# Layer norm of a transformer block moved to ScalarE, in program order, with earlier requests for the tokens

## The chip, the cores and the metric

The kernel runs on one core of a Trainium2 chip. The core has TensorE (matrix products, called PE in the profile; PEld are its weight loads), VectorE (DVE), ScalarE (ACT), GpSimd (POOL) and SyncE (SP, which issues most of the transfers). Each engine works through its own list of instructions in order and waits on semaphores for the others. The metric is the device time of one execution in microseconds (us), lower is better.

## The reference

One block of a diffusion transformer, in fp32, on 2 rows of 2048 tokens with 512 features, 16 heads, and 2048 hidden features of the MLP. A condition vector gives each row six modulation vectors.

```
mod = silu(condition) @ Wada + bada
sh_a, sc_a, gt_a, sh_m, sc_m, gt_m = split(mod, 6)
xn = layernorm(x, g1, be1)
xm = xn * (1 + sc_a) + sh_a
x  = x + gt_a * (causal_attention(xm @ Wqkv) @ Wproj + bproj)
xn = layernorm(x, g2, be2)
xm = xn * (1 + sc_m) + sh_m
x  = x + gt_m * (gelu(xm @ W1 + b1) @ W2 + b2)
```

`layernorm` subtracts each token's mean over the 512 features, divides by the root of the variance plus 1e-5, and applies g and be.

## The kernel before, in words

The work runs in stages, and for the two rows one after the other: QKV of row 0, attention of row 0, projection of row 0, then the same for row 1, then the MLP of both rows. In the profiled execution QKV of row 0 takes the time from about 20 to 200 us, its attention to 740, its projection to 799, row 1's QKV to 997, its attention to 1530, its projection to 1590, and the MLP the rest. A stage does some work of the next beside its own, through hooks called `between(n)` after each product `n`.

**Tokens on their way to QKV.** A tile `x` holds 128 tokens by 512 features; four tiles make a group of 512 tokens, and a row has four groups. The pool of a row's `x` tiles has four buffers, so one group's. `load_x` requests the four tiles of a group on SP's queue. `stats` runs two VectorE instructions for a tile (L215, L218: mean and variance into `mv`). After the fourth, `inv_std` makes `rstd` of a group: a root on ScalarE (L221), a reciprocal on VectorE (L222). `norm(g, j)` takes the two tiles of half `j` of group `g`: it normalizes each in place on VectorE (L244, subtract the mean, multiply by `rstd`), transposes the 128 x 128 blocks on TensorE into PSUM banks `ps_xt` (L211), and writes them with scale and shift of the modulation into `xmT` (L263 on VectorE, L268 on ScalarE, by turns). The reference's normalized and modulated tokens are then in `xmT`, features along the partitions.

**The products of a QKV group.** `Qkv.group` runs 12 products: eight for queries and keys (n = 0 to 7; a q and a k product for each quarter of the features), four for values (n = 8 to 11). After a q or k product ScalarE writes a rounded copy `hl` of the result (L833), VectorE the remainder (L834), and SP stores both parts to DRAM (`q<-hl`, `k<-hl`, L839). The text calls these two instructions the split. `hl` has four buffers; one comes free when its store has landed. After a value product ScalarE copies the result to `vv` (L855). Products and transposes take their PSUM banks from one pool of six.

**What runs beside it.** From the second group on, scores of the first units of attention are computed among the products (matmuls into `s`, from `qst` and `kst`, which SP loads back from the stores), and VectorE takes their maxima (`mx`, L456 and L461). `s` has two banks, so a score matmul waits for the maximum taken from the bank it will fill. In row 1's QKV stage GpSimd also prepares the MLP's weights (`w`, `w1e`, `w2d`), with loads and stores of its own.

**What sets the order.** Instructions wrapped in `act(...)` or `mm(...)`, matrix products and transposes among them, keep the order of the program on their engine. All others a scheduler places on their engine, ahead of or behind these, when it expects their operands. The normalizes of `norm` are not wrapped, and of the statistics only those called with `keep`. When group `g` runs, `between` requests group `g + 1`'s tokens at n = 0 (unless already there) and calls `norm(g + 1, 0)` at n = 5 and `norm(g + 1, 1)` at n = 8. In row 0 for every group after the first, and in row 1 for its third and fourth, `norm(g, 0)` runs the four statistics ahead of the normalizes. Row 1's first two groups have theirs from the projection of row 0.

**Hooks of the two projections.** `project_phase` runs 16 products of a row's attention output with Wproj. While row 0's runs, its hook makes row 1's first group ready: statistics at n = 0 to 3, `norm` at n = 5 and 8. While row 1's runs, the hook makes the first two groups of the MLP ready: `ln_t` (normalize and transpose, with `mv2` and `rstd2`) at n = 5, 7, 11 and 13. These tiles carry the name `qst` in the profile. The MLP's later groups are normalized on ScalarE already (L1281, `xn<-x,shift,rstd`), with `shift2` = -mean x rstd made at the end of `project_phase` (L1064).

The call that puts everything the scheduler does for a group into one place:

```
def norm(self, g, j):
    if j == 0:
        if g > b:
            for t in range(MTT):
                self.stats(g, t)
        self.xmT[g] = ...
    return transposed(...)
```

Of the kernel before, what the change touches and what calls it, by code (L numbers as in the profile page):

```python
# [17 lines left out]
P = 128  # L18
# [9 lines left out]
def dit_block_kernel(  # L28
# [36 lines left out]
    nc = tc.nc  # L65
# [82 lines left out]
    rstd1 = const.tile([P, B * NT], F32, tag="rstd1", name="rstd1")  # L148
    mv2 = const.tile([P, B * NT, 2], F32, tag="mv2", name="mv2")
    rstd2 = const.tile([P, B * NT], F32, tag="rstd2", name="rstd2")  # L150
    shift2 = const.tile([P, B * NT], F32, tag="shift2", name="shift2")

    bgate = bp.tile([P, D], F32, tag="bgate", name="bgate")
# [51 lines left out]
    def act(ins):  # L205

        return tc.keep_in_program_order(ins)
# [9 lines left out]
            act(ins)  # L217
        nc.vector.bn_aggr(mv[:, n, :], st)  # L218

    def inv_std(mv, rstd, lo, hi):  # L220
        nc.scalar.activation(rstd[:, lo:hi], mv[:, lo:hi, 1], AF.Sqrt, bias=eps)  # L221
        nc.vector.reciprocal(rstd[:, lo:hi], rstd[:, lo:hi])  # L222

    def rows_of(psum, r, b, tag):

# [1 line left out]
        mm(ps, pick[:, r, b, :], modr, start=True, stop=True)  # L227
        return ps

    def transposed(pool_, psum, xts, n0, mv, rstd, a, c, b, dst, xns=None):  # L230

        count = len(xts)
        per = 512 // (count * P)
        by_act = xns is not None
        xns = xns or []
        for t, xt in enumerate(xts):
            if by_act:  # L240
                continue
            xn = xt
            n = n0 + t
            nc.vector.tensor_scalar(  # L244
                xn, xt, mv[:, n, 0:1], rstd[:, n : n + 1], ALU.subtract, ALU.mult
            )
            xns.append(xn)
        banks = []
        for cc in range(0, C, per):
            ps = psum.tile([P, per, count * P], F32, tag="mm", name="ps_xt")  # L250
            for ci in range(per):
                for t in range(count):
                    transpose(
                        ps[:, ci, t * P : (t + 1) * P],
                        xns[t][:, (cc + ci) * P : (cc + ci + 1) * P],
                    )
            banks.append(ps)

        def modulate(chunks=range(C)):
# [12 lines left out]

        return modulate
# [498 lines left out]
    class Qkv:  # L772
# [20 lines left out]
        def stats(self, g, t, keep=False):  # L793

            n0 = self.row.b * NT + g * MTT
            stats(self.qp, self.xts[g][t], n0 + t, mv1, keep)
            if t == MTT - 1:
                inv_std(mv1, rstd1, n0, n0 + MTT)

        def norm(self, g, j):  # L800

            b = self.row.b
            if j == 0:
                if g > b:
                    for t in range(MTT):
                        self.stats(g, t)
                self.xmT[g] = self.qp.tile([P, C, MT], F32, tag="xmT", name="xmT", bufs=2)
            return transposed(
                self.qp, self.psum, self.xts[g][2 * j : 2 * j + 2],
                b * NT + g * MTT + 2 * j, mv1, rstd1, a1, c1, b,  # L810
                self.xmT[g][:, :, j * 2 * P : (j + 1) * 2 * P],
            )

# [45 lines left out]
        def run(self, hp, also):  # L859

            row = self.row
            for g in range(NG):

                def between(n):
                    if g + 1 < NG:
                        if n == 0 and g + 1 not in self.xts:
                            self.load_x(g + 1)
                        if n in (5, 8):
                            self.norm(g + 1, n // 8)()
                    elif n == 8:  # L870

                        row.rows(0)
                        act(nc.scalar.activation(first, eps, AF.Exp))
                    also(g, n)

                def among(n, k):
                    if g > 0 and n >= 2:


                        past = 4 * (n - 2) + k + 1  # L880
                        if g == 1:
                            row.score(row.count(cum[0] * past / 40, 0))
# [119 lines left out]
    def project_phase(row, psum, between):  # L1002
# [5 lines left out]
        with pool(f"proj{b}") as pp:  # L1008
# [51 lines left out]
                    between(n)  # L1060
                    n += 1
        lo, hi = b * NT, (b + 1) * NT
        inv_std(mv2, rstd2, lo, hi)
        nc.vector.scalar_tensor_tensor(  # L1064
            shift2[:, lo:hi], mv2[:, lo:hi, 0], -1.0, rstd2[:, lo:hi], ALU.mult, ALU.mult
        )


    row = Row(0)
    with pool("wada") as wp, pool("qkv0") as qp, pool(  # L1070
# [87 lines left out]

        for t in range(MTT):
            qkv.stats(0, t)  # L1160
        halves = [qkv.norm(0, 0)]

        act(
# [3 lines left out]
        )  # L1167
        picks()
        columns = modulation(0)
        halves.append(qkv.norm(0, 1))  # L1170
        columns()
        scale_shift(a1, c1, r_g1, r_be1, 0, 1)
# [36 lines left out]
    with pool("qkv1") as qp, pool("ps_qkv1", bufs=6, space=PSUM) as ps_mm:  # L1209
        qkv = Qkv(row, qp, ps_mm)  # L1210
        qkv.xts[0] = past.next_s

        def between(n):
            if n == 6:
                qkv.load_w(nc.gpsimd)

            if n < MTT:
                qkv.stats(0, n, True)
            if n in (5, 8):
                qkv.norm(0, n // 8)()  # L1220
            if n == 8:
                qkv.load_x(1)
            if n >= NT - MTT:
                qkv.stats(1, n - (NT - MTT), True)

        project_phase(past, ps_mm, between)

        with pool("hl1") as hp:
            late = FirstLayer(hp)

            def also(g, n):
                if quarters.at <= FC:
                    if n % 2 == 1:
                        quarters.step()
                elif n % 2 == 0:
                    late.step()

            def rooms():
                w = hp.tile([P, 7, C * P], F32, tag="w49", name="w7", bufs=2)
                w = w.rearrange("p n d -> p (n d)")  # L1240
                return [w[:, k * piece : (k + 1) * piece] for k in range(2)]

            quarters.more_rooms = rooms
            qkv.run(hp, also)
            assert quarters.at >= FC and late.at == 7 and not late.rooms
# [8 lines left out]
    with ExitStack() as mlp:  # L1254
# [8 lines left out]
        ]  # L1263
        sx = {}

        def ln_t(m, g, j, xts, xns=None):

            n0 = (2 * m + g) * MTT + 2 * j
            transposed(
                wp, ps_mm, xts, n0, mv2, rstd2, a2, c2, n0 // NT,  # L1270
                xm[:, :, g, j * half_t : (j + 1) * half_t], xns,
            )()

        def normed(m, n, xts):
# [106 lines left out]
        def between(n):  # L1381
            if n == 4:
                gate_columns()
            if n in (6, 7):
                wts.load(0, n - 6)
            if n in (5, 7):
                j = n // 7
                ln_t(0, 0, j, row.next_s[2 * j : 2 * j + 2])
                for t in (2 * j, 2 * j + 1):
                    nc.sync.dma_start(row.next_s[t], x1d[MTT + t])  # L1390
            if n in (11, 13):
                j = n // 13
                ln_t(0, 1, j, row.next_s[2 * j : 2 * j + 2])
            if n == 13:
                for k in range(1, 5):
                    token_sum(k)
# [440 lines left out]
        for m in range(NM):  # L1837
# [11 lines left out]
            if m + 1 < NM:  # L1849
# [11 lines left out]
                def among(n, k):  # L1861
                    n = OUTER.index(n)
                    if n < MTT and k == 3:
                        xns.append(normed(m + 1, n, coming[0]))
                    elif n < MTT and k == 6:
                        if n + 1 < MTT:
                            coming.append(load_pair(n + 1))
                        ln_t(m + 1, n // 2, n % 2, coming.pop(0), xns.pop())
                    elif n == 6 and k >= 3:
                        assert not hid.todo  # L1870
                        token_sum(k - 2)
# [56 lines left out]
```

## Time and profile before

| | us |
|---|---|
| median of 3 runs | 2316.29 |
| lowest and highest of them | 2315.68, 2319.18 |
| the profiled execution's own time | 2323.64 |
| its span, first to last instruction | 2321.8 |

The profile is of one execution. Durations and idle times in it add up to its span, not to the median of the other runs. A row of a timeline or of a group reads: start and duration (or busy time and mean), engine, line of the code, operation, output and inputs by their names in the program, shapes, how many, and in brackets the idle time of the engine ahead of it with what ended it. A row of the waits reads: engine, tile and line that waited, then engine, tile and line it waited for, then the time in all, how often, and the longest. A row of the windows reads: the stretch, its length, then busy time and number of instructions of TensorE, weight loads, VectorE, ScalarE and GpSimd, the granted TensorE clock as a share of full speed, the share of time that the DMA engines are busy (1.00 is all 16; a little more can come out) and GB/s.

### The profile page before, as it was taken

To read this page: it belongs to the slowest core of one execution; us is meant where nothing else is said; L and a number is where in the kernel's file an instruction comes from. 1 tells how busy PE (TensorE), PEld (TensorE's weight loads), DVE (VectorE), ACT (ScalarE), POOL (GpSimd) and SP (SyncE) were. 2 spreads that over 40 slices of the span, in tenths; PEclk is the share of its full clock that TensorE was granted. 3 is DMA by queue.
4 is the path that set the end of the run, shared out by engine and by line. 5 is a ranking of instruction groups with operands and counts; after the bars stand their busy time and mean duration, and the time that the engine had idled before them with its cause. 6 is when DMAs were issued, how large, how long until landed. Compare 5 with 4: busy or idle time off the path is not lost. (4 is left out here: it accounts for less than half of the span.)

```text
span 2321.8 us, 33418 instructions
## 1 busy us (share of the span) xinstructions
PE 2262.0 (97%) x12141; PEld 1387.3 (60%) x12141; DVE 1579.0 (68%) x3117; ACT 915.0 (39%) x1744; POOL 1289.6 (56%) x1036
## 2 busy tenths in 40 slices
PE   8999999999999999999999998999999999999998
PEld 3455455455544444454455554446888888788787
DVE  3366776777756635577677777555896876876787
ACT  2112555555555011155555554622332242152230
POOL 1052987878793664468788885554663602602510
PEclk9999999999999999999999999999999999999999
DMA  7577216151224799970522304265376654654543
GB/s 254 185 243 206 56 27 134 29 119 47 84 107 144 234 301 312 330 192 24 119 47 54 89 24 138 78 218 203 119 266 214 207 178 145 202 184 155 199 143 116
DMA packets 118524, 355.60 MB, mean 153 GB/s; under 512 B 14496, under 2 KB 15052, under 8 KB 103640
## 3 DMA queue, kind: packets, MB, share of 16 engines
q1 hardware_dynamic: 107040, 293.64, 42.0%
q0 software_dynamic: 10944, 59.28, 7.0%
q8 instruction: 96, 1.57, 0.3%
q14 instruction: 68, 0.56, 0.1%
q10 hardware_dynamic: 376, 0.55, 0.1%
HBM read 253.80 MB, written 107.48 MB: 156 GB/s over the span
## 5 line engine op out<-in xcount | busy, mean ns | idle before, releaser
L596 ACT ACTIVATE e<-st 128x512 f32<-128x512 f32 (+1 forms) x1152 | 573.7, 579 | 405.5 <-PE st L203 363.6
L461 DVE TENSOR_REDUCE mx<-s 128x1 f32<-128x512 f32 x612 | 413.4, 687 | 190.3 <-PE s L203 189.1
L626 POOL TENSOR_TENSOR ee<-ee,e 128x1024 f32<-128x1024 f32 x212 | 498.8, 2384 | 12.3 <-ACT e L596 12.3
L203 PE MATMUL s<-kst,qst 128*128 128x512 f32 (+3 forms) x1032 | 473.6, 460 | 20.7 <-DVE mx L461 9.9
L203 PE MATMUL st<-qst,kst 128*128 128x512 f32 (+3 forms) x1280 | 401.9, 379 | 0.0
L203 PE MATMUL ps_a<-sum,room 128*128 128x256 f32 x1504 | 357.3, 382 | 8.8 <-DVE c L1412 6.2
L203 PEld LDWEIGHTS ps_a<-sum,room 128*128 128x128 f32 x1504 | 281.3, 190 | 58.5 <-issue 11.4
L203 PE MATMUL o<-e,vv 128*32 128x512 f32 (+3 forms) x2560 | 301.1, 539 | 0.9 <-POOL e L605 0.9
L456 DVE CUSTOM_DVE_ANT_0 junk<-s,causal 128x128 bf16<-128x128 f32 (+3 forms) x420 | 206.2, 491 | 121.8 <-PE s L203 114.1
L203 PEld LDWEIGHTS s<-kst,qst 128*128 128x128 f32 x1032 | 194.6, 189 | 154.8 <-issue 66.1
L203 PEld LDWEIGHTS st<-qst,kst 128*128 128x128 f32 x1280 | 229.5, 189 | 68.9 <-issue 39.6
L626 POOL TENSOR_TENSOR ee<-e 128x1024 f32<-128x1024 f32 x84 | 198.2, 2381 | 123.2 <-ACT e L596 123.2
L203 PE MATMUL ps_qk<-xmT,wqkv 128*128 128x512 f32 x512 | 239.0, 594 | 1.8 <-DVE xmT L263 1.8
L605 POOL TENSOR_SCALAR_AFFINE_SELECT e<-e 128x256 f32<-128x256 f32 x256 | 103.9, 435 | 112.5 <-ACT e L596 110.3
L203 PEld LDWEIGHTS ps_qk<-xmT,wqkv 128*128 128x128 f32 x512 | 93.9, 190 | 97.2 <-issue 90.9
L203 PEld LDWEIGHTS <-sel 32*128 32x128 bf16 x1152 | 29.8, 91 | 197.0 <-issue 194.9
L1640 POOL TENSOR_TENSOR c<-c,h 128x512 f32<-128x512 f32 x40 | 58.0, 1470 | 160.8 <-ACT c L1638 160.8
L203 PE MATMUL ps_b<-sum,room 128*128 128x256 f32 x608 | 143.6, 379 | 0.0
L203 PEld LDWEIGHTS ps_b<-sum,room 128*128 128x128 f32 x608 | 115.0, 190 | 15.4
L203 PE MATMUL ps_v<-wqkv,xmT 128*128 128x512 f32 x256 | 123.7, 600 | 0.0
L203 PE MATMUL st<-fold,sel 32*128 32x512 bf16 (+1 forms) x1152 | 118.5, 373 | 4.3 <-DVE mhl L482 2.8
L203 PEld LDWEIGHTS o<-e,vv 128*32 128x32 f32 x2560 | 61.3, 108 | 98.9 <-issue 80.8
(179 smaller groups left out, 2949.5 us busy)
## 6 DMA issues: line engine op xcount, KB each, us to landing
qst<-q SPq DMA_DIRECT2D x128, 256.0 KB
room<-w1e SPq DMA_DIRECT2D x28, 1024.0 KB
kst<-k SPq DMA_DIRECT2D x24, 1024.0 KB
room<-w1e SPq DMA_DIRECT2D x28, 768.0 KB
room<-w2e SPq DMA_DIRECT2D x21, 1024.0 KB
q<-hl SPq DMA_DIRECT2D x32, 512.0 KB
k<-hl SPq DMA_DIRECT2D x32, 512.0 KB
room<-w2e SPq DMA_DIRECT2D x21, 768.0 KB
```

The lines of the kernel that those rows point to most:

```text
L203: return tc.keep_in_program_order(nc.tensor.matmul(*args, **kw))
L456: nc.vector.tensor_tensor_reduce(junk[:, :w], s[:, :w], causal[:, QB - w :], 1.0, MASKED, ALU.add, ALU.max, m,)
L461: nc.vector.tensor_reduce(m, s[:, :w], axis=AX.X, op=ALU.max)
L596: act(nc.scalar.activation(e[:, h % 2, :w], sts[h][:, :w], AF.Exp))
L605: nc.gpsimd.affine_select(d, d, pattern=[[0, 2], [1, P]], compare_op=ALU.is_ge, fill=0.0, base=0, channel_multiplier=-1,)
L626: act(engine.tensor_tensor(dst, x, y, ALU.add))
L1640: nc.gpsimd.tensor_tensor(c, c, piece_of(base, i, t, pair), ALU.add)
```

## The change

- A new constant `shift1` holds -mean x rstd for the first norm. `inv_std` makes it with one more VectorE instruction for each group (for the MLP's norm the instruction that made `shift2` moves into `inv_std`).
- A new function `normalize` does what `transposed` did ahead of its transposes, wrapped in `act`. It uses ScalarE (in place, Identity with `shift` as bias and `rstd` as scale), except for row 0's first group, which stays on VectorE. So 36 of 40 normalizes change engine.
- Within a QKV group the four statistics of the next group come one after each of the products 1 to 4, wrapped too. The normalizes follow at n = 5 and 8, the transposes one product later than before, at n = 6 and 9.
- The tokens of group g + 2 are requested at n = 9 of group g, in place of n = 0 of group g + 1.
- In row 0's projection the normalizes stand at n = 4 and 7, the transposes as before at 5 and 8. In row 1's the normalizes stand at n = 4, 6, 10 and 12, the transposes as before at 5, 7, 11 and 13.
- In the MLP only the arguments of `ln_t` change.

```diff
-    def inv_std(mv, rstd, lo, hi):
+    def inv_std(mv, rstd, lo, hi, shift=None):
         nc.scalar.activation(rstd[:, lo:hi], mv[:, lo:hi, 1], AF.Sqrt, bias=eps)
         nc.vector.reciprocal(rstd[:, lo:hi], rstd[:, lo:hi])
+        if shift is not None:
+            nc.vector.scalar_tensor_tensor(
+                shift[:, lo:hi], mv[:, lo:hi, 0], -1.0, rstd[:, lo:hi], ALU.mult, ALU.mult
+            )
...
+    def normalize(xts, n0, mv, rstd, shift):
+        for t, xt in enumerate(xts):
+            n = n0 + t
+            if shift is None:
+                act(
+                    nc.vector.tensor_scalar(
+                        xt, xt, mv[:, n, 0:1], rstd[:, n : n + 1], ALU.subtract, ALU.mult
+                    )
+                )
+            else:
+                act(
+                    nc.scalar.activation(
+                        xt, xt, AF.Identity,
+                        bias=shift[:, n : n + 1], scale=rstd[:, n : n + 1],
+                    )
+                )
...
-            nc.vector.tensor_scalar(
-                xn, xt, mv[:, n, 0:1], rstd[:, n : n + 1], ALU.subtract, ALU.mult
-            )
...
         def norm(self, g, j):
             b = self.row.b
             if j == 0:
-                if g > b:
-                    for t in range(MTT):
-                        self.stats(g, t)
...
                         if n == 0 and g + 1 not in self.xts:
                             self.load_x(g + 1)
+                        if 1 <= n <= MTT and g >= row.b:
+                            self.stats(g + 1, n - 1, True)
                         if n in (5, 8):
-                            self.norm(g + 1, n // 8)()
+                            self.normalize(g + 1, n // 8)
+                        if n in (6, 9):
+                            self.norm(g + 1, n // 9)()
+                        if n == 9 and g + 2 < NG:
+                            self.load_x(g + 2)
...
+            if n in (4, 7):
+                qkv.normalize(0, n // 7)
             if n in (5, 8):
                 qkv.norm(0, n // 8)()
...
+            if n in (4, 6, 10, 12):
+                g, j = n // 10, int(n in (6, 12))
+                normalize(
+                    row.next_s[2 * j : 2 * j + 2], g * MTT + 2 * j, mv2, rstd2, shift2
+                )
```

More of the change, by code (lines that the diff above doesn't have):

```diff
@@ L150, in dit_block_kernel @@
     rstd2 = const.tile([P, B * NT], F32, tag="rstd2", name="rstd2")
+    shift1 = const.tile([P, B * NT], F32, tag="shift1", name="shift1")
     shift2 = const.tile([P, B * NT], F32, tag="shift2", name="shift2")
@@ L228, in rows_of, with transposed @@
         return ps
-    def transposed(pool_, psum, xts, n0, mv, rstd, a, c, b, dst, xns=None):
-        count = len(xts)
-        per = 512 // (count * P)
[L237 to L244, printed above, removed]
-                xn, xt, mv[:, n, 0:1], rstd[:, n : n + 1], ALU.subtract, ALU.mult
-            )
-            xns.append(xn)
+    def normalize(xts, n0, mv, rstd, shift):
[14 more added lines that the diff above has]
+                )
+    def transposed(psum, xns, a, c, b, dst, by_act=False):
+        count = len(xns)
+        per = 512 // (count * P)
         banks = []
@@ L797, in stats, with normalize @@
             if t == MTT - 1:
-                inv_std(mv1, rstd1, n0, n0 + MTT)
+                inv_std(mv1, rstd1, n0, n0 + MTT, shift1)
+        def normalize(self, g, j):
+            b = self.row.b
+            normalize(
+                self.xts[g][2 * j : 2 * j + 2], b * NT + g * MTT + 2 * j,
+                mv1, rstd1, shift1 if b or g else None,
+            )
         def norm(self, g, j):
@@ L803, in norm @@
             if j == 0:
-                if g > b:
-                    for t in range(MTT):
-                        self.stats(g, t)
                 self.xmT[g] = self.qp.tile([P, C, MT], F32, tag="xmT", name="xmT", bufs=2)
             return transposed(
-                self.qp, self.psum, self.xts[g][2 * j : 2 * j + 2],
-                b * NT + g * MTT + 2 * j, mv1, rstd1, a1, c1, b,
+                self.psum, self.xts[g][2 * j : 2 * j + 2], a1, c1, b,
                 self.xmT[g][:, :, j * 2 * P : (j + 1) * 2 * P],
@@ L1062, in project_phase @@
         lo, hi = b * NT, (b + 1) * NT
[L1063 to L1066, printed above, removed]
+        inv_std(mv2, rstd2, lo, hi, shift2)
     row = Row(0)
@@ L1160, in dit_block_kernel @@
             qkv.stats(0, t)
+        qkv.normalize(0, 0)
         halves = [qkv.norm(0, 0)]
@@ L1169, in dit_block_kernel @@
         columns = modulation(0)
+        qkv.normalize(0, 1)
         halves.append(qkv.norm(0, 1))
@@ L1264, in dit_block_kernel, with ln_t @@
         sx = {}
-        def ln_t(m, g, j, xts, xns=None):
+        def ln_t(m, g, j, xns, by_act=False):
             n0 = (2 * m + g) * MTT + 2 * j
             transposed(
-                wp, ps_mm, xts, n0, mv2, rstd2, a2, c2, n0 // NT,
-                xm[:, :, g, j * half_t : (j + 1) * half_t], xns,
+                ps_mm, xns, a2, c2, n0 // NT,
+                xm[:, :, g, j * half_t : (j + 1) * half_t], by_act,
             )()
@@ L1385, in between @@
                 wts.load(0, n - 6)
+            if n in (4, 6, 10, 12):
+                g, j = n // 10, int(n in (6, 12))
+                normalize(
+                    row.next_s[2 * j : 2 * j + 2], g * MTT + 2 * j, mv2, rstd2, shift2
+                )
             if n in (5, 7):
@@ L1867, in among @@
                             coming.append(load_pair(n + 1))
-                        ln_t(m + 1, n // 2, n % 2, coming.pop(0), xns.pop())
+                        coming.pop(0)
+                        ln_t(m + 1, n // 2, n % 2, xns.pop(), True)
                     elif n == 6 and k >= 3:
```

## The prediction

> **What bounds the kernel now.** I read the page's engine totals first, then TensorE's waits, then the windows around them, and last the instructions at each wait.
>
> ```profile
> PE 2262.0 (97%) x12141; PEld 1387.3 (60%) x12141; DVE 1579.0 (68%) x3117; ACT 915.0 (39%) x1744; POOL 1289.6 (56%) x1036
> ...
> PE 27%; DVE 4%; issue 1%; ACT 0%; DVEq 0%; ACTq 0%
> ```
>
> TensorE is busy for 97% of 2321.8 us and leads the chain that ended last. The change takes no matmul away, so it can only win what TensorE idles, 59.8 us in all, and of this only the part in stages that the change touches. VectorE's average of 68% says little; what counts is where it is late.
>
> ```profile
> 840.00:860.00 20.00, 17.85 (x46) 8.04 (x45) 9.82 (x27) 3.16 (x6) 10.69 (x17) 1.00 0.99 310
> 860.00:880.00 20.00, 20.00 (x66) 10.33 (x64) 7.27 (x23) 4.41 (x8) 13.47 (x20) 1.00 1.05 314
> 880.00:900.00 20.00, 17.39 (x45) 8.11 (x44) 10.98 (x32) 3.63 (x7) 7.44 (x11) 1.00 0.85 273
> 900.00:920.00 20.00, 20.00 (x64) 10.66 (x63) 13.74 (x34) 3.41 (x6) 7.69 (x8) 1.00 0.92 303
> 920.00:940.00 20.00, 17.21 (x51) 8.95 (x50) 11.12 (x29) 3.18 (x6) 10.02 (x10) 0.91 1.03 364
> ...
> PE s L203 <- DVE mx L461: 5.4, 2, 2.8
> PE s L203 <- DVE mx L456: 2.1, 1, 2.1
> ```
>
> The windows give TensorE, weight loads, VectorE, ScalarE and GpSimd busy time, then the granted clock, the DMA share and GB/s; the last two rows are TensorE's waits from 795 to 1005 us, the QKV stage of row 1. It has three holes of 2.15, 2.61 and 2.79 us, and in each a score matmul waits for a maximum on VectorE. The other windows are full. In row 0's QKV stage no such hole stands: there the change has nothing to win, only room to lose.
>
> **The change part by part.** *Statistics one a product, and no normalize on VectorE.* The first two holes:
>
> ```profile
> 847.44 0.69 DVE L215 BATCH_NORM_STATS2 stat<-x 128x6 f32<-128x512 f32 x1 [9.05 <-DMA x<-in_x_dram]
> 848.05 0.67 DVE L834 SCALAR_TENSOR_TENSOR hl<-ps_qk,hl 128x512 fp32r<-128x512 f32 x1
> 850.90 0.69 DVE L215 BATCH_NORM_STATS2 stat<-x 128x6 f32<-128x512 f32 x1 [0.58 <-DMA x<-in_x_dram]
> 852.66 0.44 PE L203 MATMUL s<-kst,qst 128*128 128x384 f32 x1 [2.15 <-DVE mx L456]
> ...
> 891.42 0.60 ACT L833 ACTIVATE hl<-ps_qk 128x512 fp32r<-128x512 f32 x1 [2.90 <-PE ps_qk L203]
> 892.21 0.69 DVE L215 BATCH_NORM_STATS2 stat<-x 128x6 f32<-128x512 f32 x1 [5.18 <-DMA x<-in_x_dram]
> 895.42 0.67 DVE L834 SCALAR_TENSOR_TENSOR hl<-ps_qk,hl 128x512 fp32r<-128x512 f32 x1
> 896.22 1.92 DVE L244 TENSOR_SCALAR x<-x,mv,rstd 128x512 f32<-128x512 f32 x4
> 899.39 0.50 PE L203 MATMUL s<-kst,qst 128*128 128x512 f32 x1 [2.61 <-DVE mx L461]
> ```
>
> VectorE runs in order. All four statistics stood ahead of the maxima, waited up to 9.05 us for tokens still landing, and held up the split's second half (L834) and then the maxima. In the second hole four normalizes (1.92 us) stood in the way too. After the change one statistic (672 ns, below) with its aggregate follows each of products 1 to 4, and the normalizes are gone from VectorE. The last tokens landed at 850.9, about two products into the group; the fourth statistic now stands behind product 4. At worst the first statistic still waits a moment. I take both holes as closed: 2.15 + 2.61 = 4.76 us. Bounds: 0 (the tokens land later still) and 4.76.
>
> *The token loads.* Though asked for at product 9, in row 1 they stay in the same place of SP's queue: behind the two last q and k stores of a group, ahead of the next group's first. These stores depend on two splits that ScalarE reaches only after the values' copies. So for row 1 nothing changes: 0. In row 0 they move ahead of one q store, where no hole is.
>
> *The third hole.*
>
> ```profile
> 896.12 0.38 SPq L839 DMA_DIRECT2D q<-hl  x1
> 905.05 0.33 SPq L325 DMA_DIRECT2D qst<-q  x1
> 918.00 0.66 SPq L839 DMA_DIRECT2D k<-hl  x1
> ...
> 932.07 1.02 PE L203 MATMUL ps_v<-wqkv,xmT 128*128 128x512 f32 x2
> 933.91 0.60 ACT L833 ACTIVATE hl<-ps_qk 128x512 fp32r<-128x512 f32 x1 [3.98 <-DMA k<-hl]
> 934.53 0.69 DVE L834 SCALAR_TENSOR_TENSOR hl<-ps_qk,hl 128x512 fp32r<-128x512 f32 x1 [3.69 <-ACT hl L833]
> 935.88 0.64 PE L203 MATMUL s<-kst,qst 128*128 128x512 f32 x1 [2.79 <-DVE mx L461]
> 936.31 1.91 PE L203 MATMUL ps_v<-wqkv,xmT 128*128 128x512 f32 x2
> ```
>
> Here a split on ScalarE waited 3.98 us for its buffer, whose store, issued at 918.00, landed 16 us later; VectorE's half waited behind it and the maxima behind that. Besides the 2.79 us, matmuls then ran at nearly half speed (1.91 us for two against 1.02), and the window's clock is 0.91: 0.09 x 17.21 us of TensorE work = 1.6 us. Together 4.4 us.
> [...]
>
> Does it close? The group's first store (896.12) goes out when L834 is through. Its split began at 891.42 and ended at 892.02, but L834 came at 895.42, behind the statistics: 3.4 us too late. Without them the store goes 3.4 us earlier, the query load behind it (905.05, which waits for that store's landing) too, and the store of 918.00 likewise, if SP's other waits follow. But with the second hole closed TensorE comes to this place 2.61 us earlier as well, so of the 3.98 us wait some 3.2 would remain. What it holds up changes: on ScalarE the second normalize of the second pair now stands behind this very split, so a transpose is reached 0.6 + 0.81 us after the buffer is free, about where product 9 has ended (933.1 - 2.61 = 930.5; buffer at 933.91 - 3.4 = 930.5): a hole of 1.4 us where 2.79 stood, probably too short for the slow clock. With the DMA share between 0.85 and 1.05 throughout, an earlier store may also land no sooner. Bounds 0 and 4.4; I take half, 2.2, near the 1.4 that the hole itself loses by these rows, with part of the clock's 1.6.
>
> *Normalizes on ScalarE.*
>
> ```profile
> 810.80 0.60 ACT L833 ACTIVATE hl<-ps_qk 128x512 fp32r<-128x512 f32 x1 [2.84 <-PE ps_qk L203]
> 814.23 0.60 ACT L833 ACTIVATE hl<-ps_qk 128x512 fp32r<-128x512 f32 x1 [2.84 <-PE ps_qk L203]
> ...
> L244 DVE TENSOR_SCALAR qst<-qst,mv,rstd 128x512 f32<-128x512 f32 x12 | 20.3, 1710 | 9.7 <-DMA qst<-x1d 9.7
> L244 DVE TENSOR_SCALAR x<-x,mv,rstd 128x512 f32<-128x512 f32 x28 | 14.5, 564 | 0.3
> L1281 ACT ACTIVATE xn<-x,shift,rstd 128x512 f32<-128x512 f32 x24 | 18.2, 812 | 0.0
> L833 ACT ACTIVATE hl<-ps_qk 128x512 fp32r<-128x512 f32 x64 | 37.8, 596 | 151.2 <-PE ps_qk L203 130.3 <-issue 17.0 <-DMA k<-hl 4.0
> L855 ACT COPY vv<-ps_v 128x512 f32<-128x512 f32 x32 | 18.7, 585 | 148.3 <-PE ps_v L203 148.3
> L215 DVE BATCH_NORM_STATS2 stat<-x 128x6 f32<-128x512 f32 x28 | 18.7, 672 | 17.1 <-DMA x<-in_x_dram 17.0
> 852.52 0.17 DVE L222 RECIPROCAL rstd<-rstd 128x4 f32<-128x4 f32 x1
> ```
>
> 36 of the 40 leave: 24 of the token form at 564 ns and 12 of the other at 1710 ns, 34.1 us of VectorE. They become 36 x 812 = 29.2 us of ScalarE, the MLP's norm being the same operation. ScalarE has them beside 3.2 to 4.4 us of other work in these windows of 20. After a product its chain is a split and two normalizes, 596 + 2 x 812 = 2.22 us, or with a copy of the values 2.81; a product lasts 3.43 us (the two splits' starts). The transposes now stand one product later, so the chain fits: 0. If a copy comes between without cover, each of the 12 pairs of the two QKV stages costs 0.585 us, 7 us as an upper bound.
> [...]
>
> Each group's new shift (128 x 4) is priced by the reciprocal of that shape, 0.17 us; 8 of them, seven beside TensorE work, the first ahead of the first transposes: 0 to 0.17, taken 0.1.
>
> *The projections.*
>
> ```profile
> 760.00:770.00 10.00, 9.39 (x29) 4.63 (x28) 10.00 (x5) 0.00 (x0) 9.29 (x9) 1.00 1.01 369
> 759.32 9.81 DVE L244 TENSOR_SCALAR qst<-qst,mv,rstd 128x512 f32<-128x512 f32 x3
> 760.83 0.98 PE L211 MATMUL ps_xt<-ident,qst 128*128 128x128 f32 x7 [0.61 <-DVE qst L244]
> ```
>
> In row 0's projection three normalizes took 9.81 us on VectorE; TensorE lost 0.61 us to the first, and nothing to the longest, since the products' banks covered it. ScalarE was idle there and normalizes one product earlier: 0.6 won, bounds 0 and 0.61. In row 1's projection no wait of TensorE names a normalize: 0.
>
> *What follows.* GpSimd's weight chain of this stage is bound by DMA and does not shorten, so attention begins closer to it:
>
> ```profile
> 991.84 0.58 POOL L999 DMA_DIRECT2D w1e<-w  x1 [0.30 <-DVE mx L461]
> 998.45 0.40 POOL L605 TENSOR_SCALAR_AFFINE_SELECT e<-e 128x256 f32<-128x256 f32 x1 [6.03 <-ACT e L596]
> ```
>
> It has 6.03 us of slack before attention's first masks. A stage 7 us shorter eats that and 1 us: I count 1.3 us against the change for this and for small new waits on ScalarE (bounds 0 and 4).
>
> Sum: 4.76 + 2.2 + 0.6 - 0.1 - 1.3 = 6.2 us saved. The profiled execution took 2323.64 us (span 2321.8), so it would take 2317.4; it lies 7.35 above the median of the runs, 2316.29, from which the forecast is 2310.1.
>
> **The rivals.**
> *The third hole stays, as a wait of the transposes.* Speaks for it: the DMA share of 1.03 and the split's place ahead of a normalize. Against: a store that goes 3.4 us earlier. Saved are 4.76 + 0.6 - 0.1 - 1.3 = 4.0: 2312.3.
> *The statistics wait as before.* They still stand in VectorE's order, and the loads haven't moved in row 1's queue; if tokens land five products into a group, the holes only move. Against: they landed within two. Time: 2316.3 - 0.5 = 2315.8.
> *Slower: ScalarE held by a store.* With VectorE free, products run up to the four split buffers; a split that waits 3.98 us for a landing, as in the third hole, then holds two normalizes behind it, and the transposes and the whole next group with them. It decides once the wait exceeds the slack of one product, 3.43 us less the 2.22 chain. Two such waits in row 1 cost 2 x (3.98 + 1.6) = 11.2, less the 5.3 won: 2316.3 + 5.9 = 2322.2. For it: the one wait seen, DMA near full. Against: only one in two whole stages.
>
> **How the numbers follow.** Forecast 0.50, third hole stays 0.25, statistics wait 0.10, slower 0.15. About 0.2%, 4.6 us, is what a measurement of this kernel can tell from no change: faster means below 2311.7, slower above 2320.9. The forecast's own range is 2306.5 (all three holes gone, costs nil: 4.76 + 4.4 + 0.6 = 9.8) to 2313; 0.06 of it lies above 2311.7 and goes to no change, 0.04 of the second case to faster. So 0.48 faster, 0.37 the same, 0.15 slower. The range takes one microsecond below that, since the median of the runs is itself known to about so much, and above it the cases without gain and part of the slower one: 2305.5 to 2318.
>
> **What would show it.** Right: from 840 to 940 us the three windows with 17 us of TensorE turn full; statistics wait less than 1 us each; the split's buffer wait is gone; the clock stays 1.00. Wrong: a wait of a transpose for ScalarE's normalize, a split waiting for a store in another group, or the holes again beside the statistics. If attention's first masks stand behind GpSimd's weight work by over 2 us, the last cost was too small.

## The result, and the profile after

The changed kernel takes 2305.66 us (median of 6 runs, 2304.09 to 2306.30) against 2316.12 before (6 runs): a ratio of 0.9953, 95% interval 0.9940 to 0.9965. That is 10.5 us where 6.2 were forecast; 0.9953 of the 2316.29 that the forecast started from is 2305.4, 0.1 us below the low end of its range, 2305.5. Its profiled execution took 2305.74 us, span 2304.0.

The windows of the changed kernel (columns as before):

```profile
840.00:860.00 20.00, 20.00 (x53) 9.41 (x52) 9.74 (x29) 3.28 (x6) 10.61 (x16) 1.00 0.91 309
880.00:900.00 20.00, 19.36 (x51) 9.29 (x50) 8.53 (x24) 2.96 (x5) 7.87 (x11) 1.00 0.84 292
920.00:940.00 20.00, 19.94 (x61) 10.36 (x60) 11.62 (x32) 5.63 (x10) 7.66 (x8) 1.00 0.85 317
...
980.00:1000.00 20.00, 18.02 (x76) 9.43 (x74) 13.08 (x30) 6.76 (x14) 14.66 (x19) 0.92 0.94 286
```

All three holes are gone, with the clock at 1.00; only 0.64 us are idle from 880 to 900. But the last window, with 19.88 us of TensorE and a clock of 1.00 before, now has a hole and a slower clock. The groups of the changed kernel from 795 to 1005 us say why the first closed:

```profile
L216 DVE BATCH_NORM_STATS2 stat<-x 128x6 f32<-128x512 f32 x10 | 6.8, 678 | 0.0
L849 ACT ACTIVATE hl<-ps_qk 128x512 fp32r<-128x512 f32 x32 | 18.9, 596 | 74.8 <-PE ps_qk L204 69.1 <-DMA q<-hl 3.7 <-DMA k<-hl 1.0
L247 ACT ACTIVATE x<-x,shift,rstd 128x512 f32<-128x512 f32 x12 | 9.2, 807 | 0.0
```

No statistic waits for its tokens any more. A split still waits for a store, once 3.7 us, without a hole at TensorE. And why the new one opened (TensorE's waits from 980 to 1040, then GpSimd's and TensorE's instructions there):

```profile
PE o L204 <- POOL e L617: 4.2, 3, 1.6
...
996.00 0.58 POOL L1021 DMA_DIRECT2D w1e<-w  x1 [0.30 <-DVE mx L468]
996.59 2.91 POOL L617 TENSOR_SCALAR_AFFINE_SELECT e<-e 128x256 f32<-128x256 f32 x8
...
997.06 2.27 PE L204 MATMUL o<-e,vv 128*32 128x512 f32 x8 [1.20 <-POOL e L617]
```

Row 1's attention needs its masks (L617), and GpSimd comes to them only after its last weight block, at 996.59. Before, it was through at 992.42, and waited 6.03 us for the first exponentials.

The largest piece lies elsewhere. These are windows of the kernel before, inside row 1's attention, with VectorE's and TensorE's instructions there; the prediction has no term for them:

```profile
1410.00:1420.00 10.00, 7.37 (x69) 4.03 (x69) 4.60 (x9) 5.17 (x10) 3.86 (x2) 1.00 0.91 335
1420.00:1430.00 10.00, 8.26 (x32) 4.29 (x32) 8.72 (x15) 3.37 (x7) 5.51 (x3) 0.66 0.32 116
1430.00:1440.00 10.00, 7.45 (x47) 3.55 (x50) 9.07 (x15) 4.67 (x10) 5.22 (x3) 1.00 0.22 82
...
1418.62 2.47 DVE L244 TENSOR_SCALAR qst<-qst,mv,rstd 128x512 f32<-128x512 f32 x1 [3.15 <-DMA qst<-x1d]
1421.74 0.26 PE L522 MATMUL ps_m<-ident_h,mhl 128*128 128x128 bf16 x1 [4.37 <-DVE mx L461]
1423.53 0.53 DVE L244 TENSOR_SCALAR qst<-qst,mv,rstd 128x512 f32<-128x512 f32 x1
1431.50 3.79 DVE L244 TENSOR_SCALAR qst<-qst,mv,rstd 128x512 f32<-128x512 f32 x2
1435.55 0.50 PE L203 MATMUL s<-kst,qst 128*128 128x512 f32 x1 [2.55 <-DVE mx L456]
```

The scheduler had put four unpinned normalizes of the MLP's norm here, between the maxima. The first waited 3.15 us for its tokens from DRAM and then took 2.47. TensorE lost 4.37 and 2.55 us, and the clock fell to 0.66 for ten microseconds, which I estimate at 0.34 x 8.26 = 2.8 us: 9.7 us together. In the changed kernel the same windows are full:

```profile
1420.00:1430.00 10.00, 10.00 (x62) 5.00 (x62) 7.52 (x18) 6.07 (x13) 10.00 (x6) 1.00 0.41 158
1430.00:1440.00 10.00, 10.00 (x66) 4.56 (x65) 7.14 (x17) 5.50 (x11) 10.00 (x6) 1.00 0.26 102
```

### The profile page after: what moved, and what is told of

Read it like the earlier page. It is cut to its first block, busy times and chain, and to the rows that moved or that the text cites. A ratio compares the mean times of both kernels' runs of the same rounds, so it can differ in the third digit from the quotient of the medians.

```text
span 2304.0 us, 33430 instructions
## 1 busy us (share of the span) xinstructions
PE 2257.0 (98%) x12141; PEld 1385.4 (60%) x12141; DVE 1544.9 (67%) x3089; ACT 940.6 (41%) x1780; POOL 1290.5 (56%) x1036
## 5 line engine op out<-in xcount | busy, mean ns | idle before, releaser
L204 PEld LDWEIGHTS s<-kst,qst 128*128 128x128 f32 x1032 | 193.9, 188 | 143.4 <-issue 65.2
L617 POOL TENSOR_SCALAR_AFFINE_SELECT e<-e 128x256 f32<-128x256 f32 x256 | 103.7, 438 | 94.4 <-ACT e L608 92.3
```

The source lines that it names most:

```text
L204: return tc.keep_in_program_order(nc.tensor.matmul(*args, **kw))
L617: nc.gpsimd.affine_select(d, d, pattern=[[0, 2], [1, P]], compare_op=ALU.is_ge, fill=0.0, base=0, channel_multiplier=-1,)
```

## The experiments

Times are medians; each ratio is to the kernel before on the same chip. To see where time goes, five marks cut a profile into stretches: the first product of row 0's projection, the last value product of row 1, the last output product of row 1's attention, the first `ps_a<-sum` product of the MLP, the end. They are the first and last starts in the tiles' view, here for the kernel before (again), the changed kernel, and the row 1 hook alone:

```profile
L203 PE MATMUL ps_o<-kst x128: 592/592/697, 739.9 to 1558.9; 128*128 128x512 f32 x128
L203 PE MATMUL ps_v<-wqkv,xmT x256: 590/592/648, 48.1 to 991.8; 128*128 128x512 f32 x128
L203 PE MATMUL o<-e,vv x2560: 272/592/1063, 224.1 to 1529.2; 128*32 128x512 f32 x137, 128*32 128x384 f32 x21, 128*32 128x256 f32 x20, 128*32 128x128 f32 x19
```

```profile
L204 PE MATMUL ps_o<-kst x128: 592/592/697, 739.1 to 1547.5; 128*128 128x512 f32 x128
L204 PE MATMUL ps_v<-wqkv,xmT x256: 590/592/648, 47.2 to 985.8; 128*128 128x512 f32 x128
L204 PE MATMUL o<-e,vv x2560: 272/592/1061, 222.8 to 1517.8; 128*32 128x512 f32 x137, 128*32 128x384 f32 x21, 128*32 128x256 f32 x20, 128*32 128x128 f32 x19
```

```profile
L204 PE MATMUL ps_o<-kst x128: 592/592/697, 738.9 to 1544.6; 128*128 128x512 f32 x128
L204 PE MATMUL ps_v<-wqkv,xmT x256: 590/592/648, 47.1 to 990.2; 128*128 128x512 f32 x128
L204 PE MATMUL o<-e,vv x2560: 272/592/617, 223.1 to 1515.0; 128*32 128x512 f32 x137, 128*32 128x384 f32 x22, 128*32 128x256 f32 x20, 128*32 128x128 f32 x18
```

Subtracting them (991.8 - 739.9 = 251.9, and so on) gives, in us:

| kernel | to projection 0 | to last values, row 1 | attention of row 1 | to the MLP | MLP | median | ratio |
|---|---|---|---|---|---|---|---|
| before, as first profiled | 739.2 | 256.3 | 534.5 | 65.1 | 726.7 | 2316.29 | |
| before_again | 739.9 | 251.9 | 537.4 | 65.2 | 720.7 | 2316.95 | 1.0002 |
| changed | 739.1 | 246.7 | 532.0 | 65.2 | 721.0 | 2305.66 | 0.9953 |
| after_again | 738.4 | 246.8 | 530.9 | 65.1 | 721.1 | 2303.97 | 0.9952 |
| row1_hook | 738.9 | 251.3 | 524.8 | 65.1 | 720.9 | 2303.27 | 0.9945 |
| row1_hook_again | 739.0 | 256.3 | 524.8 | 65.1 | 721.0 | 2303.46 | 0.9951 |
| qkv_alone | 740.2 | 247.1 | 541.0 | 65.1 | 720.8 | 2316.10 | 0.9998 |
| stats_group | 742.7 | 252.7 | 525.5 | 65.2 | 721.0 | 2306.41 | 0.9940 |
| loads_before | 742.0 | 246.5 | 529.2 | 65.1 | 720.9 | 2304.18 | 0.9953 |
| all_dve | 745.5 | 261.6 | 525.1 | 66.6 | 720.9 | 2320.60 | 1.0023 |
| transposes_5_8 | 757.1 | 265.3 | 525.1 | 65.2 | 720.7 | 2335.65 | 1.0066 |
| quarters_early | 755.0 | 250.5 | 525.1 | 65.1 | 720.7 | 2313.48 | 0.9977 |
| row1_early | 753.3 | 258.1 | 524.9 | 65.1 | 720.9 | 2325.85 | 1.0031 |
| quarters_two | 739.2 | 251.2 | 525.0 | 65.1 | 720.7 | 2302.89 | 0.9945 |

The stretches are of one profiled execution each, so a row need not add up to the median.

**The kernel before, once more.** No edit.

> The kernel before once more, for its profile. Theory A (the change won at separate places, one of them four normalizes of the MLP's norm that stood on VectorE among the maxima of row 1's attention): TensorE again loses about 7 us between 1410 and 1440 us to VectorE's mx behind L244, with a granted clock well under 1.00 there, and the span is 2314 to 2318 us, since the 6.2 us wait for c (L1412) in the MLP was an accident. Rival B (the hole at 1417 was an accident of the one profiled execution): TensorE is full from 1410 to 1440. The time is within 0.1% of before by both.

The attention hole is there again (4.4 and 2.5 us, clock 0.77 from 1410 to 1440). The clock cost more this time, by the same estimate 0.23 x 23.10 = 5.3 us, because it fell behind the second wait too (TensorE's instruction and its window):

```profile
1432.08 0.80 PE L203 MATMUL s<-kst,qst 128*128 128x512 f32 x1 [2.54 <-DVE mx L456]
1430.00:1440.00 10.00, 7.92 (x32) 3.73 (x32) 6.63 (x12) 3.39 (x7) 2.89 (x2) 0.66 0.27 103
```

The MLP's 726.7 of the first profile were not: 720.7. Of the 7.35 us by which that execution lay above the median, 6 stood in the MLP. The third hole of the QKV stage is missing too. Interval of the ratio: 0.9992 to 1.0012.

**The row 1 hook alone, and all but it.** In `row1_hook` the QKV stages and row 0's projection are as in the kernel before. In `qkv_alone` this part is undone:

```diff
-            if n in (4, 6, 10, 12):
-                normalize(row.next_s[...], ..., mv2, rstd2, shift2)
...
+            if not by_act:
+                for t, xt in enumerate(xns):
+                    nc.vector.tensor_scalar(xt, xt, mv2[...], rstd2[...], ALU.subtract, ALU.mult)
```

> The kernel before with one part of the change alone: the MLP norm's normalizes on ScalarE at n = 4, 6, 10 and 12 of row 1's projection. Theory A: 7 to 10 us faster than before (2306 to 2309), with TensorE full from 1410 to 1440, and the three holes of row 1's QKV still there. Rival B: no change, within 1 us.

> The changed kernel without that part: row 1's projection has its normalizes unpinned on VectorE as before, all else is changed. Theory A: the 8.9 us won in row 1's QKV stage and 0.8 in the projection ahead of it are mostly given back at attention's start, where GpSimd ends its weight work later, so 1 to 4 us faster than before (2312 to 2315). Rival B: about 10 us faster (2306), the same as the whole change.

The hook alone gives 0.9945 (0.9933 to 0.9956), as much as the whole change or more; all the rest gives 0.9998 (0.9986 to 1.0010). Row 1's attention falls from 534.5 or 537.4 us to 524.8 with the hook. Without it, and with the QKV edits, it takes 541.0, more than before. Rival B falls: the hole is the kernel's, and it is the change's gain.

**All normalizes on VectorE, pinned at the same places.**

```diff
-            if shift is None:
+            if True:
                 act(nc.vector.tensor_scalar(...))
```

> The changed kernel with all 40 normalizes on VectorE at the same places of the program, pinned. Theory C (the place in the order counts, not the engine): within 2 us of the changed kernel (2305 to 2308). Rival D (VectorE's load counts): each pair's 1.1 us stands ahead of the maxima in the three groups of row 1 and opens waits of 1 to 2 us at TensorE again, 4 us or more slower than the changed kernel (2310 or more).

Slower than the kernel before: 1.0023 (1.0010 to 1.0036), 15 us over the changed one. Rival D, 4 us or more, holds. TensorE's waits from 740 to 1005:

```profile
PE ps_xt L212 <- DVE x L241: 4.2, 2, 3.3
PE s L204 <- DVE mx L468: 3.4, 2, 3.1
PE s L204 <- DVE mx L473: 2.0, 2, 1.4
PE ps_xt L212 <- DVE qst L241: 1.5, 2, 1.1
```

Transposes wait for normalizes and scores for maxima, and the clock is 0.91 in two windows (840 to 860 and 940 to 960 us). Attention is 525.1 here, so the pin alone cures its hole, on either engine. In the QKV stages the pinned order does not do on VectorE. It is not simply full: it is busy for 13.94 of 20 us from 940 to 960. But some normalizes beside GpSimd's own arithmetic take longer. Here are two that take 3.67 us, where the median of the kernel's 28 on tokens is 0.54, with GpSimd's instructions at that time and the wait behind them:

```profile
940.80 3.67 DVE L241 TENSOR_SCALAR x<-x,mv,rstd 128x512 f32<-128x512 f32 x2
939.05 5.13 POOL L988 TENSOR_TENSOR w<-w 128x512 f32<-128x512 f32 x4
945.59 0.50 PE L204 MATMUL s<-kst,qst 128*128 128x512 f32 x1 [3.06 <-DVE mx L468]
```

In the changed kernel all 36 on ScalarE take 0.80 to 0.83 us. That GpSimd is the cause is argued from the times; no run takes its arithmetic away from beside them. The waits shown are 11.1 us; 6.4 us more go ahead of row 0's projection, where the largest wait for a normalize is 3.0.

**Weight steps moved out of row 1's QKV stage.** GpSimd does four, or two, more steps in row 0:

```diff
-            if g == NG - 1 and n % 2 == 0:
+            if g == NG - 1 and n % 2 == 0 or g == NG - 2 and n in (5, 7, 9, 11):
                 quarters.step()
```

(with `n in (9, 11)` for two; `row1_early` is the row 1 hook alone with four).

> The changed kernel with four of GpSimd's weight steps moved from row 1's QKV stage into the third group of row 0's, where the DMA share is 0.7. Theory G (what the change wins in row 1's QKV stage is given back because GpSimd's weight chain there ends 10 us behind the last values and holds attention's first masks): the last w1e store goes out well before the last value product, TensorE's waits for POOL e (4.7 us from 995 to 1040) vanish, and the time is 2297 to 2301. Rival H (GpSimd only covers another delay, such as DMA traffic or the maxima): the waits move to another engine, and the time stays at 2304 to 2307.

> The kernel before with the row 1 hook alone and the same four weight steps moved. Theory G: there GpSimd was late by little, so 2301 to 2304, within 2 us of the row 1 hook alone, and slower than the changed kernel with the steps moved by the 3 to 5 us that the QKV edits are worth. Rival H: the moved steps change nothing or help both alike.

With four, attention of row 1 is 525.1 as theory G has it, but the total misses (2313.48): GpSimd is now late for row 0's masks, one wait of 10.8 us (TensorE's waits from 235 to 740):

```profile
PE o L204 <- POOL e L617: 11.2, 2, 10.8
```

`row1_early` (2325.85, where 2301 to 2304 was expected) has the same wait (12.7 us in all) and a hole of 7.9 in row 1's QKV stage, where unpinned statistics again wait for tokens.

> The changed kernel with two of GpSimd's weight steps, not four, moved into row 0's QKV stage. In the run with four, GpSimd reached row 0's first masks 20 us later than in the changed kernel (236.16 against 216.36), and in row 1's attention nothing waited for it. Theory G: with two, GpSimd reaches row 0's masks at about 218, 2 us late at most, and row 1's masks wait for nothing: 7 us of row 1's attention come back, 0 to 2 go in row 0, so 2297 to 2301, faster than either part alone. Rival H (row 1's QKV stage is held by its transfers, so the products wait elsewhere once GpSimd is out of the way): 2304 to 2308.

With two, neither attention waits for GpSimd (0.4 us each), and row 1's is 525.0. But the stretch to the last values takes 251.2 in place of 246.7: a maximum is late again, and the clock is 0.91 in that window. The maximum stood behind the change's own new instruction on VectorE, `shift`, which took 3.68 us beside GpSimd's arithmetic (its median in this run is 0.17):

```profile
914.37 0.50 PE L204 MATMUL s<-kst,qst 128*128 128x512 f32 x1 [2.08 <-DVE mx L473]
...
900.00:920.00 20.00, 17.93 (x53) 9.57 (x51) 16.19 (x36) 4.03 (x7) 7.73 (x8) 0.91 1.02 326
...
910.03 3.68 DVE L225 SCALAR_TENSOR_TENSOR shift<-mv,rstd 128x4 f32<-128x4 f32 x1
909.97 5.07 POOL L988 TENSOR_TENSOR w<-w 128x512 f32<-128x512 f32 x4
```

So theory G is right on what held attention. Rival H's time fits better than G's, but its reason, a stage held by transfers, is not shown: this wait is the new instruction's. The time, 2302.89, is within the intervals of the changed kernel and of the hook alone on the same chip.

**Parts of the QKV edits.** Statistics unpinned at n = 5; transposes back at n = 5 and 8; tokens requested at n = 0 of the next group:

```diff
-                        if 1 <= n <= MTT and g >= row.b:
-                            self.stats(g + 1, n - 1, True)
+                        if n == 5 and g >= row.b:
+                            for t in range(MTT):
+                                self.stats(g + 1, t)
...
-                        if n in (6, 9):
-                            self.norm(g + 1, n // 9)()
+                        if n in (5, 8):
+                            self.norm(g + 1, n // 8)()
...
-                        if n == 9 and g + 2 < NG:
-                            self.load_x(g + 2)
```

> The changed kernel with the four statistics of a group unpinned at n = 5 again. Theory: the first two holes (2.2 and 2.6 us) come back, since the statistics and not the normalizes held VectorE; row 1's QKV ends 4 to 5 us later, but as GpSimd's chain holds attention's start anyway, the time is the same or better, 2303 to 2307. Rival (the QKV edits count in full): 2309 to 2311.

One hole, of 4.6 us, is back in row 1's QKV stage, where two were expected; the stretch takes 252.7 in place of 246.7. The statistics wait for tokens again, and the split and the maximum behind them are late (the statistics' group from 795 to 1005, and TensorE's wait):

```profile
L216 DVE BATCH_NORM_STATS2 stat<-x 128x6 f32<-128x512 f32 x11 | 7.5, 682 | 15.9 <-DMA x<-in_x_dram 15.8
902.46 0.51 PE L204 MATMUL s<-kst,qst 128*128 128x512 f32 x1 [4.64 <-DVE mx L473]
```

Attention then is 525.5 in place of 532.0, and the total is the changed kernel's (2306.41, ratio 0.9940, 0.9927 to 0.9953).

> The changed kernel with the transposes of a QKV group at n = 5 and 8 as before, right behind their normalizes on ScalarE. Theory: without the product between, each of the 12 pairs waits for a split and two normalizes (2.2 us less what the banks cover, so 1 to 2 us), in row 0 too: 10 to 20 us slower than the changed kernel. Rival (the cover isn't needed): within 1 us.

Ratio 1.0066 (1.0053 to 1.0080), 30 us slower than the changed kernel, more than expected. Each of the 12 pairs, six for row 0 and six for row 1, waits twice, once for each of its tiles (20 to 200 us and 740 to 1005 us):

```profile
PE ps_xt L212 <- ACT x L247: 10.7, 12, 1.9
PE ps_xt L212 <- ACT x L247: 10.6, 12, 1.5
```

That is 21.3 us, about 1.8 for a pair. The first two stretches are longer by about 18 each than in the changed kernel, and attention gives 6.9 back. Three windows of 20 us there have a clock of 0.91, by the same estimate about 1.6 us each; what the rest is stays open.

> The changed kernel with the tokens requested at n = 0 of the next group, as before. In SP's queue only row 0's requests move, behind one q store and the weights of bproj. Theory: no change, within 1 us of the changed kernel. Rival (the earlier request is what closes holes): 3 us or more slower, with statistics waiting for x.

2304.18 beside 2303.97 of the changed kernel on the same chip: no difference shows.

**The two side by side.** No edits.

> The changed kernel once more, on the same chip as the next. Theory A with G: 2305 to 2307; the QKV edits cost 1 to 4 us net beside the row 1 hook alone, because attention's start gives back more than the QKV stage wins. Rival (the QKV edits are worth nothing either way, and 2303.3 against 2305.7 was the difference of two chips): within 1 us of the row 1 hook alone.

> The kernel before with the row 1 hook alone, once more. Theory A with G: 2302 to 2304, 1 to 4 us below the changed kernel run beside it. Rival: within 1 us of it.

2303.97 and 2303.46, so the rival holds: no worth of the QKV edits shows either way, within the 2.8 us that each ratio is uncertain by, and the 2.4 us between 2305.66 and 2303.27 can't be called a difference of the kernels.

**Without the stores of w1e.**

```diff
+    for n in range(7):
+        nc.sync.dma_start(w1e[n], x[0, : 7 * P, :].rearrange("(p n) d -> p n d", n=7))
     attention_phase(row)
...
-            act(nc.gpsimd.dma_start(w1e[n], room))
```

> The changed kernel without the seven stores of w1e in row 1's QKV stage; w1e is filled with other data earlier, so the MLP's first layer works on other weights. This takes 13 MB of the stage's 65 MB away, and the waits for their landing from GpSimd's chain. From the first product of row 0's projection to the last value product of row 1 the changed kernel took 247 us, and from there to the last output product of row 1's attention 531 to 532. Theory G: GpSimd is ready in time, so 247 and 525. Rival H (something else holds attention's start): 247 and 530 or more.

> The kernel before with the row 1 hook alone, and the same stores left out. With them it took 251 to 256 us and 525. Theory G: 525 stays, and the stage keeps its holes at the statistics, so it is 250 to 256; against the same edit of the changed kernel 4 to 9 us slower: the QKV edits pay once the traffic is gone. Rival (fewer transfers close the holes by themselves): 247 to 248 and 525, no difference between the two.

The marks of the changed kernel without the stores, then of the hook alone without them:

```profile
L204 PE MATMUL ps_o<-kst x128: 592/592/697, 740.8 to 1542.2; 128*128 128x512 f32 x128
L204 PE MATMUL ps_v<-wqkv,xmT x256: 590/592/648, 48.3 to 987.6; 128*128 128x512 f32 x128
L204 PE MATMUL o<-e,vv x2560: 272/592/618, 224.4 to 1512.6; 128*32 128x512 f32 x137, 128*32 128x384 f32 x21, 128*32 128x256 f32 x20, 128*32 128x128 f32 x19
```

```profile
L204 PE MATMUL ps_o<-kst x128: 592/592/697, 740.0 to 1547.3; 128*128 128x512 f32 x128
L204 PE MATMUL ps_v<-wqkv,xmT x256: 590/592/648, 48.2 to 992.7; 128*128 128x512 f32 x128
L204 PE MATMUL o<-e,vv x2560: 272/592/617, 224.2 to 1517.6; 128*32 128x512 f32 x137, 128*32 128x384 f32 x21, 128*32 128x256 f32 x20, 128*32 128x128 f32 x19
```

246.8 and 525.0 against 252.7 and 524.9: with the stores gone attention waits 0.4 us for GpSimd in either kernel, and the QKV edits keep their 5.9 us in these stretches. In these two profiles 0.8 us of it are lost ahead of row 0's projection and 1.2 in the MLP (722.3 against 721.1). The median times are 2301.03 and 2304.08. The intervals of their ratios (0.9917 to 0.9947, 0.9927 to 0.9960) overlap, so the 3 us between them are a sign and no proof; the stretches are one execution each.

## Why the prediction was right or wrong

- **First two holes**: right. Statistics spread over four products no longer wait, and TensorE's loss there is gone. `stats_group` shows that their place does it (it undoes the spreading and the pin together). Their size is not steady: the first was 2.15, 1.74, 0.27 and 1.78 us in the four profiles with unedited QKV stages.
- **Third hole**: it closed, but it was not a steady part of the kernel. Of the four profiles with unedited QKV stages on the same stores, it stands in two (256.3 us for the stretch) and not in the others (251.3, 251.9). Taking half of 4.4 was about right on average, by luck: the prediction took half because it doubted that the hole closes.
- **Token loads**: right as far as the times can tell, zero.
- **Normalizes on ScalarE**: right that the chain fits behind one product. A split did wait 3.7 us for a store, more than the slack of 3.43 - 2.22 = 1.2 us from which the rival was to decide, and TensorE was idle for no more than 0.06 us in the two windows around it; so the feared loss did not come, though the wait did. Without the product's cover the kernel is 30 us slower, and each of 12 pairs waits about 1.8 us; the prediction's upper bound of 7 us was for a lesser case, a copy in between. A normalize of tokens takes longer on ScalarE (807 ns in row 1's QKV stage of the changed kernel) than on VectorE (580 in that stage of the kernel before, 542 for row 0's first group of the changed one), but with all of them on VectorE this kernel is 15 us slower (`all_dve`). In engine time it is no loss: 12 of the 36 had taken 1710 ns on average, so by the prediction's rows 34.1 us of VectorE become 29.2 of ScalarE.
- **The new shift**: its 0.17 us is right as a median, but in `all_dve` one took 2.97 us and in `quarters_two` one took 3.68, with a hole behind it. The two profiles of the changed kernel had no such hole: its longest of this shape took 0.37 and 0.82.
- **Row 0's projection**: right by the first profiles; 0.6 us were forecast, row 1's first QKV product starts at 796.06 in place of 796.86, and no wait for a normalize is left. The wait isn't steady: the second profile of before has none, and the second of the changed kernel has one of 0.4 for ScalarE's normalize.
- **Row 1's projection: this is the step that failed.** "In row 1's projection no wait of TensorE names a normalize: 0." True of the projection, but four of the eight normalizes did not stand there. Unpinned and ready once their tokens were loaded, they had been placed 100 us earlier, among attention's maxima, where TensorE's waits name the maxima and not the normalize. Price: 9.7 us in the first profile, 12.6 by the stretches of the second. The list of TensorE's waits for the whole run shows it (ps_m waiting 4.4 us for mx), and the view of tile qst gives the place.
- **What follows**: mis-sized. 1.3 us were counted; attention's start lost 532.0 - 524.8 = 7.2. Of these 4.2 are waits for GpSimd and, by the clock of 0.92, 0.08 x 18.02 = 1.4 an estimate of the clock's part; the remaining 1.6 stay open. GpSimd's chain did not merely stay: it ended 4 us later (996.59 against 992.42), and 2 us later in the second profiles (995.07 against 993.07). It is the prediction's own sign that the last cost was too small: masks behind GpSimd's weight work by over 2 us.
- **The sum**: against the second profile of before, the changed kernel saves 0.8 ahead of row 0's projection (where the kernels' first profiles differ by 0.1), 251.9 - 246.7 = 5.2 from there to the last values, 537.4 - 532.0 = 5.4 in attention (12.6 less 7.2), and loses 0.3 in the MLP: 11.1, beside the 10.5 measured. That the forecast had the right sign was luck: its gain is in the wrong place, and what it counted on, the QKV stage, is given back whole.
- **The profile's own time**: moving the difference over to the median was right, since its 7 us extra were an accident of the MLP.

What stays open: why GpSimd's chain ends later once the QKV stage is quicker. From 795 to 1000 us its waits for loaded weights grow from 31.8 to 35.6 us (31.5 to 35.2 in the second profiles), those for the stores of w1e do not (42.7 and 42.6), and the DMA share is 0.84 to 1.04 in the changed kernel's windows of 20 us from 800 on; that earlier q and k stores take the transfers' time is argued, not shown.

## What to carry to other kernels

Where a scheduler places unpinned work, look for every instruction that an edit touches by its tile over the whole run, not in the stage where the code has it: here the wait that it caused carried another name (`ps_m` waiting 4.4 us for `mx`). Then ask of each stage what else must be ready at its end; here a stage made shorter than GpSimd's weight work gave the time back at the next one's start. Here a normalize pinned ahead of the product that hides it cost nothing on ScalarE, 15 us on VectorE and 30 us without the product.

## What the runs showed of the hardware that was not expected

- The same normalize on VectorE (128 x 512) took 0.53 us at 1423.53, 2.47 at 1418.62, and 7.03 at the longest, in row 0's projection. The slow ones stand beside GpSimd's arithmetic: that of 1418.62 ends at 1421.09, GpSimd's two TENSOR_TENSOR that began at 1416.14 end at 1420.80, and none ran at 1423.53. The 3.68 us of `shift` in `quarters_two` fit this too. No run takes GpSimd's arithmetic away from beside them, so the cause is not shown.
- In the first profile the granted clock fell to 0.66 over ten microseconds behind a hole of 4.37 us, and kept 1.00 behind holes of 2.55 and 2.61. But it was 0.91 over 20 us behind 2.79 us in the same profile, 0.66 over ten behind 2.54 us in `before_again` and 0.91 over 20 behind 2.08 us in `quarters_two`: here the length of the hole alone does not decide. That a hole of 1.4 us is too short for the slow clock, as the prediction supposed, was its author's estimate; no run shows where it starts.
- By the estimates above the clock's loss was nearly a third of the attention hole's price in the first profile, 2.8 of 9.7 us, and more in the second, 5.3 of 12.6.
